# Joining layer 0's feed-forward and layer 1's attention rounds in one written program

## The chip, the core and the metric

The kernel runs on one core of one Trainium2 chip. The metric is the device time of one execution in microseconds (us). A core has five engines with a queue each: TensorE (PE in the profile; PEld is its loading of weights), VectorE (DVE), ScalarE (ACT), GpSimd (POOL) and SyncE (SP), which here mostly issues DMA transfers. Products land in PSUM, which has eight banks of 2 KB for each of the 128 partitions; everything else lies in SBUF. Shapes are written partitions x elements.

## The reference

A tensor x of 8 x 256 rows of 512 goes through two layers, each a normed attention on a context and a normed feed-forward, all added to x:

```python
x = x + _L0_xattn_ref(_layernorm(x), ctx, ctx, ...)     # retention, 4 heads
x = x + _L0_ffn_ref(_layernorm(x), w1, w2, w3)
x = x + _L1_xattn_ref(_layernorm(x), ctx, ctx, Wi, bi, Wf, bf, ln_scale)
x = x + _L1_ffn_ref(_layernorm(x), ...)                 # 32 experts, top 4, and a shared one
```

The change touches the second and the third line. The second, with hidden size 1408:

```python
def bitlinear(x, w):          # both sides rounded: x to 127 steps of its row's largest, w to -1, 0, 1
    return einsum('bsd,hd->bsh', act_quant(x), weight_quant(w))
h = silu(bitlinear(x, w1)) * bitlinear(x, w3)
return bitlinear(h, w2)
```

The third is an mLSTM of 16 heads of 32 (q is the normed x, k and v are the context):

```python
ig = (concat(q, k, v) @ Wi + bi);  fg = (concat(q, k, v) @ Wf + bf)     # one number per row and head
F = cumsum(log_sigmoid(fg))
log_D = F[s] - F[t] + ig[t]  for t <= s, else -inf;  M = max over t of log_D
C = (qh . kh / sqrt(32)) * exp(log_D - M)
h = (C / (max(|C.sum|, exp(-M)) + 1e-6)) @ vh
out = layernorm of each head of h, times ln_scale
```

## The kernel before

The 2048 rows are 16 tiles of 128 (two tiles are one of the 8 batches); x stays in SBUF as `g.X[0..15]`. `layers_kernel` (L1647) runs `layer0_attention`, then `layer1_constants` and `Gates` (weights and helpers of layer 1), `layer0_ffn`, `layer1_attention`, and `layer1_ffn` (routing and experts). The order of the work around the change is written out by hand: inside `tc.manual_schedule` the named engines get their instructions in the order of the program text (PE, ACT and DVE in the feed-forward; PE, ACT, DVE and POOL in layer 1's rounds), and other queues are ordered by a scheduler. Semaphores for data and for reused buffers are placed by the framework.

**`layer0_ffn` (L571)** loops over the 16 tiles t. Three chunks of hidden columns are 8 matmuls each (L590), into p1 and p3 (two PSUM buffers each); ACT makes silu (L598), DVE the gate (L603), its row's largest value (L607) and the rounding to bf16 (L626); a transposing DMA (L627) turns it; `output` (L632) is 11 matmuls for tile t-2; `added` (L637) puts it on x for tile t-3. For layer 1 each finished tile is then normed: `stats` (L109), an inverse root in about a dozen small DVE steps for a group of tiles (`rooted`, L89 to L102), `norm_next` on ACT (L696), four transposes on PE (`turn_next`, L704) into the bank `ft`, and a copy into `qT` (`copy_next`, L711). Groups of tiles for one root are 4, 2, 2, 4, 2, 1, 1. After the loop (L781 to L827) stands a tail: the last outputs and norms, and the gates of the later tiles.

**`Gates` (L449)** makes F, M and the rest for all rows at once, 128 pairs of batch and head on partitions. `context` (L491) multiplies the context's side in tiles 0 and 1, `queries` (L500) the side of q. `chain` (L509) is the sequence after that, for batches 0 to 3 (first) and 4 to 7 (second): products that pick the rows (L517), biases (L522, L525), log-sigmoid as Abs, Exp and Ln on ACT (L528 to L532), two scans (L537, L542), sums, then the split of two rows into three bf16 parts each (casts L552, subtractions L556), which go to DRAM (`parts_d`, L557; three `part` buffers), and a turned F (L563) whose Exp (L566) becomes `em`.

**`layer1_attention` (L861)** has 32 blocks (8 batches, 4 groups of 4 heads) and works on four at a time, one round per n (`round_`, L1102): `decays` of block n (products L909 and L910 of the operands `left` and `right` into one of two banks `dec`, then Exp L914 into `xe`, in three pieces), `back` of block n-3 (L965, copied by ACT into `hid`, L969), `weights` of n-1 (L929, L933, and DVE's product with the decays, `ct`, L937), `heads` of n-2 (L950; copy L958), and a `tail` that norms finished batches: absolute sums (L980, L981), squares on POOL (L987), variance (L993 to L995), the inverse root on DVE, scaling on POOL (L1000), `attended` on POOL (L1007, L1008: times ln_scale, added to x, one tile at a time), and later the norm for the next layer and its turned copy (`turned`, L1037, which also takes a `dec` bank). `hid` has three buffers, `xe` three. `values` (L882) loads the parts into `left` and `right` of one of two pairs, and the batch's context rows, at n % 4 == 2 for the next batch. The second chain of gates advances one step per round from round 0. Two lines that set the order of the tail of a batch (L1056 to L1060 and L1075):

```python
if r == 0: nm[b] = scales(..); sq[b] = squares(..); if b: attended(b - 1, hid.pop(b - 1), (1,))
if r == 3: ...; scaled(hid[b], rs); attended(b, hid[b], (0,) if b + 1 < B else (0, 1))
```

Block r of batch b here means round n = 4b + 6 + r.

Of the kernel before, what the change touches and what calls it, by code (L numbers as in the profile page):

```python
# [19 lines left out]
F32 = mybir.dt.float32  # L20
# [40 lines left out]
MAGIC = 12582912.0  # L61

# [386 lines left out]
class Gates:  # L449
# [4 lines left out]
    def __init__(self, g, wp):  # L454
        self.g = g
        nc = g.nc
        self.bif = wp.tile([P, 2], F32, tag="bif", name="bif")
# [8 lines left out]
        self.em = wp.tile([P, 2, P], F32, tag="em", name="em")  # L466
        self.parts = [wp.tile([P, S], BF16, tag=f"part{n}", name=f"part{n}") for n in range(3)]
# [4 lines left out]
        self.fg, self.af, self.ig, self.F, self.gg, self.M = (row() for _ in range(6))  # L472

# [10 lines left out]
    def open(self, ps):  # L484
        self.pg = ps.tile([P, CH], F32, tag="pg", name="pg", bufs=1)

    def context(self, of):

        for k in of:
            for c in range(NCH):  # L490
                self.g.nc.tensor.matmul(  # L491
                    self.pg[c * 2 * H1 : (c + 1) * 2 * H1, :], lhsT=self.Wkv[:, k, :], rhs=self.g.ctxT[c][:, k, :],
                    start=k == 0, stop=False,
                )

    def queries(self, of):

        for k in range(KD):
            for c, cols in of:
                self.g.nc.tensor.matmul(  # L500
                    self.pg[c * 2 * H1 : (c + 1) * 2 * H1, cols], lhsT=self.W[:, k, :], rhs=self.g.qT[c][:, k, cols],
                    start=False, stop=k == KD - 1 and cols.stop == CH,
                )

    def kept(self, h):
        rows = slice(h * 64, (h + 1) * 64)
        self.g.nc.vector.tensor_copy(self.gs[rows], self.pg[rows])

    def chain(self, h, two, turned, fine=False, each=False):  # L509
# [12 lines left out]
        nc.vector.tensor_scalar(fg, both[r, 1], self.bif[r, 1:2], None, ALU.add)  # L522
        if each:
            yield
        nc.vector.tensor_scalar(ig, both[r, 0], self.bif[r, 0:1], None, ALU.add)  # L525
        yield

        nc.scalar.activation(af, fg, AF.Abs)  # L528
        nc.scalar.activation(af, af, AF.Exp, scale=-1.0)
        if each:  # L530
            yield
        nc.scalar.activation(af, af, AF.Ln, bias=g.ones[r, 0:1])  # L532
        yield
        nc.vector.scalar_tensor_tensor(fg, fg, 0.0, af, ALU.min, ALU.subtract)
        if each:
            yield
# [3 lines left out]
        if each:  # L540
            yield
# [3 lines left out]
        if each:  # L545
            yield
        nc.vector.tensor_scalar(M, M, -1.0, None, ALU.mult)
        yield

        for n, rest in enumerate((gg, M)):  # L550
            for m, part in enumerate(self.parts):
                nc.vector.tensor_copy(part[r], rest)  # L552
                if each and m < 2:
                    yield
                if m < 2:
                    nc.vector.tensor_sub(rest, rest, part[r])  # L556
                (nc.sync if n or h else nc.scalar).dma_start(out=g.parts_d[n, m, r], in_=part[r])  # L557
                if (fine or each) and m < 2:
                    yield
            yield  # L560
# [6 lines left out]

# [3 lines left out]
def layer0_ffn(g, tc, gates):  # L571
# [5 lines left out]
    with tc.tile_pool(name="f0work", bufs=2, reuse_waits="tile") as work, tc.tile_pool(name="f0ps", bufs=2, space=PSUM, reuse_waits="tile") as ps:  # L577

        xq, h, p, am, inv, sc, hq, hqT, py, mv, var, roots, rs, nb, xn, ft = ({} for _ in range(16))

        def products(t, n):
            a, z = chunks[n]
            xqT = xq[t][0]
            if n == 0:
                h[t] = work.tile([P, FF], F32, tag="h", name="h")
            p1 = ps.tile([P, 512], F32, tag="p1", name="p1")
            p3 = ps.tile([P, 512], F32, tag="p3", name="p3")
            for pp, w in ((p1, w1), (p3, w3)):
                for k in range(KD):
                    nc.tensor.matmul(  # L590
                        pp[:, : z - a], lhsT=xqT[:, k, :], rhs=w[:, k, a:z], start=k == 0, stop=k == KD - 1
                    )
            sg = work.tile([P, 512], F32, tag="sg", name="sg")
            p[n] = p1[:, : z - a], p3[:, : z - a], sg[:, : z - a]
# [23 lines left out]
        def hidden_scale(t):  # L618
# [3 lines left out]
            hqT[t] = work.tile([P, NF, P], BF16, tag="hqT", name="hqT", bufs=3), s2  # L622

        def hidden_rounded(t):
            hq = work.tile([P, FF], BF16, tag="hq", name="hq")
            nc.vector.tensor_scalar(hq, h.pop(t), MAGIC, 127.0, ALU.subtract, ALU.min)  # L626
            nc.sync.dma_start_transpose(out=hqT[t][0], in_=hq)  # L627

        def output(t):
            py[t] = ps.tile([P, D], F32, tag="py", name="py")  # L630
# [8 lines left out]
        def input_normed(i):  # L639
            xn[i] = work.tile([P, D], F32, tag="y", name="xn")  # L640
# [8 lines left out]
        def input_rounded(i):  # L649
            q = work.tile([P, D], BF16, tag="xq", name="xq")  # L650
# [5 lines left out]
        groups = [range(4), range(4, 6), range(6, 8), range(8, 12), range(12, 14), range(14, 15), range(15, 16)]  # L656
# [3 lines left out]
        def stats(i):  # L660
            of = group[i]
            if i == of[0]:
                mv[of] = work.tile([P, 4, 2], F32, tag="mv4", name="mv4")
# [4 lines left out]
        def centers(of):  # L668
            m = len(of)
            v = work.tile([P, 4], F32, tag="var4", name="var4")[:, :m]  # L670
# [4 lines left out]
            nb[of] = work.tile([P, 4], F32, tag="nb4", name="nb4")[:, :m]  # L675
# [3 lines left out]
        def rooted(i, n):  # L679
            for _ in range(n):  # L680
                next(step.get(group[i], iter(())), None)

        def woven(i, others):
            for _ in others:
                rooted(i, 1)
            rooted(i, NT)
# [3 lines left out]
        def norm_next():  # L690
            if normed:
# [3 lines left out]
                y = work.tile([P, D], F32, tag="xn1", name="xn1")  # L695
# [3 lines left out]
        def turn_next(tag="ft", bufs=1):  # L699
            if turns:  # L700
                i, y = turns.pop(0)
                pt = ps.tile([P, KD, P], F32, tag=tag, name="ft", bufs=bufs)
# [4 lines left out]
        def copy_next():  # L707
            if copies:
                i, pt = copies.pop(0)
                c, o = divmod(i * P, CH)  # L710
                nc.scalar.copy(g.qT[c][:, :, o : o + P], pt)  # L711
                return i

        with tc.manual_schedule(engines={E_.PE, E_.Activation, E_.DVE}):
# [3 lines left out]
            gates.open(ps)  # L718
            at_py = lambda: ps.tile([P, 2, S], F32, tag="py", name="gates")
            first = gates.chain(0, at_py, at_py, each=True)  # L720

            for t in range(NT):
                front = t - 3
                if t:
# [6 lines left out]
                silu(t, 0)  # L731
                if t:
                    shifted(("h", t - 1), h[t - 1])
                gated(t, 0)
                if t + 2 < NT:
                    input_scale(t + 2)
                if front >= 0:
                    stats(front)
                    rooted(front, 2)
                products(t, 1)  # L740
                if t == NT - 1:
                    next(first)
# [3 lines left out]
                if front >= 0:  # L746
                    rooted(front, 3)
# [3 lines left out]
                if front >= 0:  # L751
                    rooted(front, 2)
                if t < 2:
                    gates.context(range(2 * t, 2 * t + 2))
                products(t, 2)
                silu(t, 2)
                if t == NT - 1:
                    for _ in range(4):
                        next(first)
                if t + 2 < NT:  # L760
                    input_rounded(t + 2)
                if front >= 0:
                    rooted(front, 2)
                turn_next()
                if t >= 2:
                    output(t - 2)
                gated(t, 2)
                if front >= 0:
                    rooted(front, NT)
                done = copy_next()  # L770
                if t + 3 < NT:
                    input_normed(t + 3)
                norm_next()
                largest(("h", t), h[t])
                if done == 7:
                    gates.queries([(0, slice(0, CH)), (1, slice(0, CH))])
                    gates.kept(0)

            last = NT - 1

            def steps(n):  # L781
                for _ in range(n):
                    yield next(first)

            hidden_scale(last)
            output(last - 1)
            turn_next()
            added(last - 2)
            shifted(("h", last), h[last])
            next(first)  # L790
            stats(last - 2)
            copy_next()
            norm_next()
            turn_next("p3", 2)
            hidden_rounded(last)
            rooted(last - 2, 2)
            added(last - 1)
            rooted(last - 2, 2)
            stats(last - 1)
            copy_next()  # L800
            norm_next()
            turn_next("p3", 2)
            copy_next()
            woven(last - 2, steps(6))
            output(last)
            norm_next()
            turn_next("p3", 2)
            norm_next()
            turn_next("ft")
            copy_next()  # L810
            copy_next()
            gates.queries([(2, slice(0, CH)), (3, slice(0, 2 * P))])
            woven(last - 1, steps(5))
            norm_next()
            turn_next("p3", 2)
            copy_next()
            gates.queries([(3, slice(2 * P, 3 * P))])
            added(last)
# [910 lines left out]
```

## Time and profile before

| what | us |
|---|---|
| median of 3 runs (1099.37 to 1104.2) | 1102.18 |
| the profiled execution | 1101.73 |
| its span | 1099.9 |
| feed-forward of layer 0, to its last products | 239.8 to 370.4 |
| from there to the first decay product | 370.4 to 403.0 |
| rounds 0 to 6 | 403.0 to 435.6 |
| rounds 7 to 13 | 435.6 to 465.8 |
| rounds 14 to 31 (the last Exp begins at 535.15) | 465.8 to 538 |

The mean granted clock of TensorE is 0.96. All times inside the program count from the span's start. One profiled execution has a page with busy time by engine and by slices; its trace answers questions by stretch of time, by wait and by instruction. In a row of the timeline the first number is the start, the second the busy time, then engine, line, operation, output and inputs, shapes, the count, and in brackets the idle time before it and what ended it. In a row of waits stand the engine and line that waited, what for, and the total, the number and the longest. In a row of stretches stand the stretch, its length, the busy time of PE, PEld, DVE, ACT and POOL with instruction counts, the granted clock, the DMA share and GB/s.

### The profile page before, as it was taken

The page shows a single profiled execution, that of the slowest core. Times are in us where ns is not written, and L with a number is a line of the kernel's source. Part 1 is how long each engine was busy: PE and PEld are TensorE (multiplying, and loading weights), DVE is VectorE, ACT ScalarE, POOL GpSimd, SP SyncE. Part 2 cuts the span into 40 slices and gives each one's busy share as a digit, 9 for nine tenths or more (in the row PEclk, how much of TensorE's full clock was granted, in tenths as well). Part 3 has the DMA queues.
Part 4 walks back from the last instruction along what each step waited for, and adds up shares of the span by engine and source line. Part 5 has one row for each costly group of instructions (what it writes and reads, how often), then busy time and mean ns, then how long its engine had stood idle before and what let it go on. Part 6 is the DMA issues. An engine that isn't in the chain of part 4 may idle for free.

```text
span 1099.9 us, 14847 instructions
## 1 busy us (share of the span) xinstructions
PE 1020.0 (93%) x5226; PEld 618.8 (56%) x5226; DVE 535.0 (49%) x1504; ACT 398.4 (36%) x680; POOL 395.5 (36%) x375
## 2 busy tenths in 40 slices
PE   7979799989999888999889899999999999999994
PEld 5746366634444345566534444555666666777782
DVE  6545555468999826888842992112221221121120
ACT  4455235136677536576631101221122222212211
POOL 0144522240000300376670223554455555545522
PEclk9989899999999868899989999999999999999997
DMA  9776321013234420212122325777777788889872
GB/s 342 275 274 216 131 93 48 1 30 59 55 70 56 117 68 27 77 61 71 39 88 81 128 84 162 177 200 189 174 199 203 203 207 235 228 226 252 239 198 35
DMA packets 101748, 154.42 MB, mean 140 GB/s; under 512 B 39812, under 2 KB 42500, under 8 KB 101640
## 3 DMA queue, kind: packets, MB, share of 16 engines
q1 hardware_dynamic: 81872, 106.68, 31.0%
q0 software_dynamic: 19552, 46.60, 19.0%
q8 instruction: 43, 0.70, 0.3%
q14 instruction: 41, 0.34, 0.1%
q10 hardware_dynamic: 240, 0.10, 0.0%
HBM read 110.42 MB, written 32.96 MB: 130 GB/s over the span
## 4 chain that ended last, share of the span: by engine, by line
PE 69%; DVE 13%; DMA 6%; POOL 4%; ACT 3%; issue 3%; SPq 0%; DVEq 0%; POOLq 0%; ACTq 0%
PE po L1478 13%; PE pg L1461 12%; PE pu L1461 12%; PE pz L380 3%; PE pw L325 3%; PE pt L1518 3%; PE p L590 3%; PE py L632 2%; DVE am L607 2%; PE pqk L929 2%; DMA vc_d<-raw 2%; PE pd L909 2%; PE num L950 2%; DMA raw<-in_ctx 1%; PE po L1168 1%
## 5 line engine op out<-in xcount | busy, mean ns | idle before, releaser
L1466 DVE TENSOR_TENSOR act<-pu,sg 128x264 f32<-128x264 f32 (+22 forms) x68 | 31.9, 469 | 314.7 <-PE pu L1461 308.5
L1503 POOL DMA_INDIRECT xg<-h_d,tok_of x85 | 83.3, 980 | 198.7 <-DVE of L1513 63.6
L1522 POOL DMA_INDIRECT out_x<-eo,to x85 | 133.0, 1564 | 54.9 <-ACT eo L1560 34.5
L1478 PE MATMUL po<-w,act 128*128 128x512 f32 (+10 forms) x456 | 143.1, 489 | 0.0
L1461 PE MATMUL pg<-xT,w 128*128 128x216 f32 (+21 forms) x512 | 136.5, 410 | 0.6 <-issue 0.6
L1461 PE MATMUL pu<-xT,w 128*128 128x216 f32 (+21 forms) x512 | 133.3, 403 | 0.0
L1560 ACT ACTIVATE eo<-po,slotw 128x512 f32<-128x512 f32 (+10 forms) x114 | 65.6, 576 | 176.9 <-PE po L1478 168.5
L1461 PEld LDWEIGHTS pg<-xT,w 128*128 128x128 f32 x512 | 93.9, 191 | 34.1 <-issue 18.7
L1461 PEld LDWEIGHTS pu<-xT,w 128*128 128x128 f32 x512 | 96.8, 190 | 26.2 <-issue 5.6
L1465 ACT ACTIVATE sg<-pg 128x264 f32<-128x264 f32 (+22 forms) x68 | 28.5, 419 | 204.5 <-PE pg L1461 192.3
L1478 PEld LDWEIGHTS po<-w,act 128*128 128x128 f32 (+10 forms) x456 | 54.1, 155 | 57.4 <-issue 47.9
L590 PE MATMUL p<-wq,xqT 128*128 128x512 bf16 (+1 forms) x384 | 80.3, 362 | 5.0 <-DVE qi L611 4.6
L937 DVE SCALAR_TENSOR_TENSOR ct<-pqk,xe 128x768 f32<-128x768 f32 x64 | 58.2, 951 | 21.7 <-PE pqk L933 16.7
L590 PEld LDWEIGHTS <-xqT 128*128 128x128 bf16 x384 | 37.2, 98 | 48.4 <-issue 10.1
L1519 DVE TENSOR_TENSOR xT<-pt,nw 128x512 f32<-128x512 f32 (+12 forms) x85 | 51.1, 601 | 21.0 <-PE pt L1518 20.8
L325 PE MATMUL pw<-wg,xnT 128*128 128x512 f32 x128 | 61.1, 622 | 0.0
L380 PE MATMUL pz<-wo,wyT 128*128 128x512 f32 x128 | 57.9, 595 | 2.1 <-ACT wyT L374 2.1
L914 ACT ACTIVATE xe<-pd 128x512 f32<-128x512 f32 x96 | 55.1, 596 | 11.0 <-PE pd L910 10.0
L1518 PEld LDWEIGHTS pt<-ident,xg 128*128 128x128 f32 (+15 forms) x340 | 39.2, 140 | 24.8 <-PE po L1478 10.5
L109 DVE BATCH_NORM_STATS2 st<-x 128x6 f32<-128x512 f32 x64 | 43.8, 685 | 15.8 <-POOL x L1008 10.2
L1518 PE MATMUL pt<-ident,xg 128*128 128x128 f32 (+15 forms) x340 | 47.2, 260 | 1.4 <-DMA xg<-h_d,tok_of 0.8
L363 POOL TENSOR_TENSOR y<-y,gam 128x512 f32<-128x512 f32 x16 | 20.9, 1304 | 76.0 <-DVE y L79 72.1
(295 smaller groups left out, 1671.1 us busy)
## 6 DMA issues: line engine op xcount, KB each, us to landing
w<-in_w SPq DMA_DIRECT2D x32, 1024.0 KB
w<-in_w SPq DMA_DIRECT2D x32, 512.0 KB
wst<-in_w1T SPq DMA_DIRECT2D x8, 704.0 KB
wst<-in_w3T SPq DMA_DIRECT2D x8, 704.0 KB
wst<-in_w2T SPq DMA_DIRECT2D x6, 768.0 KB
x<-in_x SPq DMA_DIRECT2D x16, 256.0 KB
ctxT<-in_ctxT_d SPq DMA_DIRECT2D x4, 1024.0 KB
raw<-in_ctx SPq DMA_DIRECT2D x16, 256.0 KB
```

The costliest lines, as they stand in the source:

```text
L325: nc.tensor.matmul(pw, lhsT=xnT[c][:, k, o : o + P], rhs=wg[:, k, :], start=k == 0, stop=k == KD - 1)
L380: nc.tensor.matmul(pz, lhsT=wyT[:, k, :], rhs=wo[:, k, :], start=k == 0, stop=k == KD - 1)
L590: nc.tensor.matmul(pp[:, : z - a], lhsT=xqT[:, k, :], rhs=w[:, k, a:z], start=k == 0, stop=k == KD - 1)
L914: nc.scalar.activation(out, pd, AF.Exp)
L937: nc.vector.scalar_tensor_tensor(ct[:, r : r + 2, :], pqk[:, :, : S + P], 1.0 / math.sqrt(HD1), xe[:, r : r + 2, :], ALU.mult, ALU.mult,)
L1461: nc.tensor.matmul(pp[:, :n], lhsT=w[:, k, cols], rhs=xT[:, k, :n], start=k == 0, stop=k == KD - 1)
L1478: nc.tensor.matmul(po[h * at : h * at + n, :cols], lhsT=act[:, m, j * P : j * P + n], rhs=w[:, m, h * cols : (h + 1) * cols], start=m == 0 ...
L1503: nc.gpsimd.indirect_dma_start(out=xg[:n], out_offset=None, in_=h_d, in_offset=bass.IndirectOffsetOnAxis(ap=g.tok_of[:n, r, j : j + 1], ax ...
L1518: nc.tensor.transpose(pt[:, k, :n], xg[:n, k * P : (k + 1) * P], g.ident[:n, :n])
L1519: nc.vector.tensor_mul(xT, pt[:, :, :n], g.nw.unsqueeze(2).to_broadcast([P, KD, n]))
L1522: return nc.gpsimd.indirect_dma_start(out=g.out, out_offset=bass.IndirectOffsetOnAxis(ap=rows, axis=0), in_=eo, in_offset=None, compute_op ...
L1560: nc.scalar.activation(eo[:n, at : at + cols], po, AF.Copy, scale=w[r][:n, j : j + 1])
```

## The change

`layer0_ffn` and `layer1_attention` become one function, `layers_joined`, with one SBUF pool and one PSUM pool for both; the round code moves to `layer1_rounds`. POOL and SP are now ordered by hand too. What was the feed-forward's tail stands in a table of places (round, place) inside rounds 0 to 6:

```diff
+            places = {
+                (0, 0): [partial(shifted, ("h", late), h[late]), partial(output, late - 1, "back", 1)],
+                (0, 1): [partial(hidden_rounded, late), partial(added, late - 1)],
+                (1, 0): [partial(rooted, 13, 6)],
+                (1, 3): [partial(rooted, 13), partial(stats, late - 1)],
+                (1, 4): [norms],
+                (2, 1): [turned],
+                (2, 3): [partial(output, late, "back", 1), rounds.second_right],
+                (2, 4): [partial(turned, nc.vector), partial(added, late), partial(times, 1, first), norms],
+                (3, 1): [partial(times, NT, first), turned],
+                (3, 3): [partial(stats, late)],
+                (3, 4): [partial(turned, nc.vector), norms],
+                (4, 1): [turned, partial(rooted, late, 6)],
+                (4, 3): [partial(rooted, late)],
+                (4, 4): [partial(turned, nc.vector)],
+                (5, 1): [norms],
+                (5, 4): [turned],
+                (6, 1): [turned],
+                (6, 4): [lambda: gates.late((2, 3), bank("dec", "pgl", 2))],
+            }
+            def between(n, place):
+                for work_of in places.get((n, place), ()):
+                    work_of()
+                if n >= 7 and place in (2, 4):
+                    times(3 if place == 2 else 2, second)
```

Places 0 to 4 of a round lie after the first two decay pieces, after `back`, after the third piece, after `weights`, and after `heads` with the tail. `turned` in this table is one tile's transposes into a `dec` bank and its copy, by ACT or DVE. `gates.late` is the query product of tiles 8 to 15 (8 matmuls of 512 columns).

The gates: the first chain's 15 steps to the last part stand in tiles 13 (3 steps), 14 (6) and 15 (6) of the feed-forward, the rest in rounds 2 and 3. Six part buffers take the place of three. The second chain waits until round 7 and then goes five steps a round. Log-sigmoid changes its form, and the second chain has a polynomial:

```diff
-        nc.scalar.activation(af, fg, AF.Abs)
-        nc.scalar.activation(af, af, AF.Exp, scale=-1.0)
-        nc.scalar.activation(af, af, AF.Ln, bias=g.ones[r, 0:1])
-        nc.vector.scalar_tensor_tensor(fg, fg, 0.0, af, ALU.min, ALU.subtract)
+        nc.scalar.activation(af, both[r, 1], AF.Tanh, bias=self.half[r, 0:1], scale=0.5)
+        nc.vector.tensor_scalar(fg, both[r, 1], self.bif[r, 1:2], 0.0, ALU.add, ALU.min)
+        nc.vector.tensor_scalar(ig, both[r, 0], self.bif[r, 0:1], None, ALU.add)
+        if h == 0:
+            nc.scalar.activation(af, af, AF.Abs)
+            nc.scalar.activation(af, af, AF.Ln, bias=self.half[r, 1:2], scale=0.5)
+            nc.vector.tensor_add(fg, fg, af)
+        else:
+            nc.scalar.activation(af, af, AF.Abs)
+            nc.vector.tensor_scalar(af, af, -0.5, None, ALU.add)
+            nc.vector.tensor_scalar(M, af, LOG[-1], None, ALU.mult)
+            for c in LOG[-2:0:-1]:
+                nc.vector.scalar_tensor_tensor(M, M, c, af, ALU.add, ALU.mult)
+            nc.vector.scalar_tensor_tensor(fg, M, LOG[0], fg, ALU.add, ALU.add)
...
-            layer1_constants(g, wp)
             gates = Gates(g, wp)
-            layer0_ffn(g, tc, gates)
-        layer1_attention(g, tc, gates)
+            layer1_constants(g, wp)
+            layers_joined(g, tc, qp, gates)
```

The buffers: p1 and p3 become one pair `p13` of two banks in the rounds' `pqk` (released together by the gate); `output` and the gates' products take the `dec` banks, `ft` takes `num` and `pg` takes `back`. In SBUF the hidden rows use the `xe` buffers, hq and its turned copy share the `ct` buffers. The first-layer weights wq0 and wq1 are reused after the feed-forward for two `hid` buffers (three before), `em`, the third `xe` and the squares; wq2, once output 15 is done, for the second right operand, which POOL clears and fills from the first, and for ln_scale:

```diff
-                        hid[b] = work.tile([P, 2, H1, HD1 + 1], F32, tag="hid", name="hid", bufs=3)
+            hid[b] = hid_of[b % 2]
...
+    def second_right():
+        more = qp.tile([P, NF * D // 2], F32, tag="wq2", name="held2")
+        half = KD * HG * S // 2
+        nc.gpsimd.memset(more[:, :half], 0.0)
+        right = more[:, :half].bitcast(BF16).rearrange("p (k r s) -> p k r s", k=KD, r=HG)
+        nc.gpsimd.dma_start(out=right[: 3 * HG], in_=g.right[0][: 3 * HG])
...
                     if r == 0:
                         nm[b] = scales(b, hid[b])
-                        sq[b] = squares(b, hid[b], nm[b])
                         if b:
                             attended(b - 1, hid.pop(b - 1), (1,))
+                        sq[b] = squares(b, hid[b], nm[b])
```

The first right operand is filled by four ACT copies in tiles 2 to 5 instead of eight POOL DMAs and a DVE cast; `values` loads the parts ahead of the context rows. The remaining moves in the feed-forward: context products in tiles 1 and 2, root groups 4, 4, 6, 2 with their steps spread over iterations, a tile's transposes split into two places of an iteration, hidden rows 13 and 14 rounded by ACT, `kept` on ACT, outputs 13, 14 and 15 in `num` and `back`.

## The prediction

> **What bounds the kernel now.** I read the page's slices first, then busy time by stage, then the waits of the joint, then two stretches in order of time. Three of the slices' rows (27.5 us a digit):
>
> ```profile
> PE   7979799989999888999889899999999999999994
> DVE  6545555468999826888842992112221221121120
> PEclk9989899999999868899989999999999999999997
> ```
>
> TensorE is nearly always busy; the one hole in its clock is slices 14 to 16, where the feed-forward ends and the rounds begin. By stage (sums of busy us, granted clock, DMA):
>
> ```profile
> core 0: us, PE busy (x) PEld busy (x) DVE busy (x) ACT busy (x) POOL busy (x), PEclk, DMA share, GB/s
> 239.80:370.40 130.60, 122.98 (x618) 58.59 (x617) 120.16 (x296) 84.32 (x111) 5.28 (x16) 0.99 0.34 59
> 370.40:403.00 32.60, 23.56 (x99) 12.35 (x98) 19.32 (x72) 16.41 (x23) 8.02 (x12) 0.72 0.39 120
> 403.00:435.60 32.60, 29.18 (x245) 15.63 (x245) 14.80 (x22) 19.02 (x36) 1.89 (x1) 0.75 0.12 30
> 435.60:465.80 30.20, 28.00 (x297) 17.43 (x296) 26.60 (x53) 16.74 (x39) 8.60 (x6) 0.89 0.24 69
> 465.80:538.00 72.20, 68.87 (x778) 44.81 (x780) 61.07 (x128) 52.03 (x115) 48.38 (x42) 1.00 0.19 62
> ```
>
> Row one, the feed-forward: PE and DVE both near full. Row two, the joint from the last products (370.4) to the first decay product (403.0): PE is busy 23.6 us but at clock 0.72. Row three, rounds 0 to 6: clock 0.75. Row four, rounds 7 to 13: DVE already holds 26.6 of 30.2 us. Row five, rounds 14 to 31: PE holds 68.9 of 72.2 us, so a PE wait there can hardly be made up. In the joint two engines wait for each other:
>
> ```profile
> ACT xn L696 <- DVE nb L676: 7.2, 3, 3.3
> PE ft L704 <- ACT xn L696: 5.9, 4, 2.0
> DVE part L552 <- DMA parts_d<-part: 5.8, 1, 5.8
> ```
>
> That is root, norm, transpose, copy, one tile after another, with 5.8 us in which DVE waits for a part buffer. This is what the change attacks.
>
> **The feed-forward: -2.5 us.** PE waits there 7.6 us: 2.6 (context products L491, whose weights come late), 4.6 for DVE in six pieces, 0.4 for ACT. Loading the gates' weights first and moving the context products a tile later takes the 2.6. Roots spread over iterations take perhaps 1.9 of the 4.6, and two fewer transposes of 0.44 take 0.9. Against that: the first chain now stands in tiles 13 to 15 on DVE, at 0.28 (cast, scalar), 0.42 (two operands), 0.66 (scan) about 6.8 us, while the rounding of hidden rows 13 and 14 leaves DVE (2 x 0.89) and input scaling has ended for the last two tiles (about 1.5 each): 2 us too much; pairing p1 with p3 costs one silu (0.65) at a refill. Sum -2.6 -1.9 -0.9 +2 +0.7, about -2.5; from -5 to +2. Last products end at 367.9.
>
> **The joint and rounds 0 to 6: 17.5 us gained, the FFN's 2.5 included.** Round 0 needs the first chain's parts in DRAM and back. DVE writes the last cast some 2.8 us after the last products (gate 0.6, parts 1.7, a root step): 370.7. Write to read took 1.9 us (cast end 395.74, load issued 397.60), a transfer 1.8 (388.94 to 390.76, the part's write); with the issue of 0.3 to 0.5, round 0 starts at 375 and not at 403. SP must not be blocked then: tile 14's transpose (2.1 us of issue) stands ahead of these loads and is over.
> From 375 to the start of round 7: seven rounds at the undisturbed pace of 3.38 (xe of rounds 4 to 11 start at 425.48, 428.86, 432.24 and so on) are 23.7. PE's moved work: outputs 14 and 15, 2 x 2.37; eight transposes of a tile, 8 x 0.5; eight query products of 512 columns, 2.4 (eight of 512 and eight of 256 took 3.62); F's transposes 0.5: 11.6. The clock: PE is idle from about 370.5 to 375, and comes back slow as at 403 (two stretches of 4 us at 0.50): 2. One root chain that ACT waits for, now in round 1: 2.7 to 3.3 in the joint's rows, take 3. Eight tiles pass through the two banks that the decays use; a turned tile there costs PE 0.35 today (idle ahead of 502.26 and of 506.57): 2.8. Sum 43.1, so round 7 starts at 418.1 instead of 435.6. Bounds: PE alone, 35.3, gives 25 gained; today's 32.6 for these rounds with 11.6 + 3 + 2.8 on top, 50, gives 10.5.
> What hides here costs nothing: four ACT copies for eight POOL DMAs and the heads' cast, the early memsets, POOL's 128x2048 clearing for the second right operand in round 2 (an estimate of 3.8 from 0.95 for a quarter of the bytes), since DVE holds 14.8 of 32.6 us there; without that cover it costs up to 3.8. The Ln and Exp loads of round 2 (413.09 and 414.91, 1.28 each, with PE waiting 3.3) go; their place is in the 3.38.
> The Trainium skill, "ScalarE: Activation LUTs", "What ACT_TABLE_LOAD costs", gives about 2.66 us a switch, a drain included; here the next activation starts 0.02 us after a load of 1.28 and I see no drain. By the page the two loads would be worth 5.3 us, by the row 2.6.
>
> **Rounds 7 to 13: 6.4 us lost.** The second chain is no longer spread from round 0: all of it stands in rounds 7 to 11, with a polynomial in place of Exp and Ln. On DVE: five scalar steps 1.4, eight polynomial steps 3.4, one sum 0.4, scans 1.3, two more 0.8, parts 3.4: 10.8, of which the parts (3.4) stand in this window today. So 26.6 + 7.4 = 34.0 us of DVE; with 2.6 us of gaps (3.6 today) 36.6 against 30.2. Lower bound 3.8 (no gaps). Upper bound 9: DVE's steps also stretch beside POOL, which this window shows:
>
> ```profile
> 448.22 1.96 POOL L1000 TENSOR_TENSOR hid<-hid,rsq 128x1024 f32<-128x1024 f32 x1 [12.65 <-DVE rsq L102]
> 448.44 2.02 DVE L556 TENSOR_TENSOR sw<-sw,part 64x256 f32<-64x256 f32 x1
> ```
>
> The subtraction that takes 0.42 elsewhere took 2.02 beside POOL's product. That now can strike any of 28 steps.
>
> **Rounds 14 to 31: 17 us lost.** Three hid buffers become two. The copy into batch b+2's first block (round 4b+11) must then wait until POOL has added batch b's second tile. Batch 3 today:
>
> ```profile
> 500.94 1.91 POOL L1000 TENSOR_TENSOR hid<-hid,rsq 128x1024 f32<-128x1024 f32 x1
> 502.94 1.18 POOL L1007 TENSOR_TENSOR hid<-hid,lns 128x512 f32<-128x512 f32 x1
> 503.29 0.38 ACT L969 COPY hid<-back 128x264 f32<-128x264 f32 x1
> 504.19 1.19 POOL L1008 TENSOR_TENSOR x<-x,hid 128x512 f32<-128x512 f32 x1
> 505.33 1.90 POOL L987 TENSOR_TENSOR sq<-hid 128x1024 f32<-128x1024 f32 x1
> 507.19 1.18 POOL L1007 TENSOR_TENSOR hid<-hid,lns 128x512 f32<-128x512 f32 x1
> 508.44 1.19 POOL L1008 TENSOR_TENSOR x<-x,hid 128x512 f32<-128x512 f32 x1
> ```
>
> Today the copy of 503.29 is batch 5's and goes to a third buffer. With two it waits for batch 3's last add. The change puts that tile ahead of the squares, so the add ends at 505.4 + 2.4 = 507.85 and not 509.6: ACT stands 4.55 us. Behind the copy on ACT: the third Exp, the head's copy, the turned tile's copy, the next round's Exps. PE goes on with weights, heads and the turned tile (to 505.9); then both decay banks are held, and the next decay product waits for the third Exp to end, 507.95 + 0.4 + 0.6 = 508.95: 3.05 us. Some comes back (DVE's 1.65 us idle at 502.9 and a slow round 24 leave about 1.2; take 0.6). The clock: after PE's pause at 453 to 456, beside POOL, it was granted 0.50 in 455 to 458 and 0.66 in 458 to 461, some 1.9 us of work lost; taken by half, 1.0. So 3.45 a batch, in rounds 15, 19, 23, 27 and 31: 17.3 (round 11's falls where DVE bounds). Bounds: 0 if POOL is done in time, 25 at 5 each.
> "TensorE: Matmul & The Clock Gate", "HAM oscillation", says in the Trainium skill that idle gaps past about 3.4 us put the clock at half. A pause of 3.05 lies just under it: by the rule 0 for the clock, or about 1.7 if the pause is a bit longer; the row's pause was near 3 and did cost clock.
>
> **After round 31** the routing and experts have the same instructions; the chain of waits there hangs on nothing that changed: 0.
>
> **Sum.** -17.5 + 6.4 + 17.3 = +6.2. The profiled execution took 1101.73 us (span 1099.9 and 1.8 around it; the median of the runs shown, 1102.18, lies 0.45 above): 1107.9, **1108**.
>
> **Rivals.**
> (A) *The third buffer isn't missed* (chance 0.25): faster. If the third Exp's bank isn't what PE needs next, or POOL's batch work starts a round earlier against PE, the wait stays on ACT and costs 1 us a batch. For: ACT holds only 52 of 72 us there. Against: PE's next instruction in order is that decay product, with two banks only. Then -17.5 + 6.4 + 5 = -6, 1096; with the full 25 of the first term 1088. It decides where a batch loses under 2.3 us.
> (B) *The joint doesn't close* (0.2): the decays' two banks, through which outputs, tiles and gates go too, make ACT and PE alternate, or the parts come late because SP or DVE is behind in tile 15. For: DVE is 95% full in the feed-forward; ACT's work in rounds 0 to 6 rises from 19 to about 28 us. Then 10 or less is gained: 1115, and with rounds 7 to 13 at 9, 1118 to 1124.
> (C) *Forecast* (0.55): all three terms near their size, 1099 to 1115, its own range.
>
> **How the numbers follow.** Half a per cent, 5.5 us, is about what a measurement of this kernel can tell from no change. Faster by more: A, 0.25. Slower: B and the upper part of C, 0.2 + 0.35 = 0.55. Within: 0.2. The range reaches from A with some of its larger gain to B: 1089 to 1124.
>
> **What would show it.** Right: the first xe near 375; round 7 at 415 to 422; DVE full in rounds 7 to 12; in rounds 15, 19, 23, 27 and 31 a wait of 4 to 5 us of ACT's hid copy for POOL, with a PE wait of some 3 us for xe after it. Wrong: no such PE wait (A); a first xe after 380, or PE waiting over 10 us in rounds 0 to 6 (B); a round of 3.4 us in 7 to 11 (the polynomial hidden).

## The result, and the profile after

The changed kernel takes 1119.12 us (median of 4 runs, 1117.76 to 1120.59), the kernel before 1103.19 (4 runs): ratio 1.0149, 95% interval 1.0115 to 1.0182. The forecast was 1108, in a range of 1089 to 1124, with 0.55 on slower: the side and the range held, and the time lies 11 us above the forecast, in the range of rival B.

The profiled execution has a span of 1118.5 us, against 1099.9. The same three rows of the page's slices (28 us a digit now):

```profile
PE   7979899989999589778798898999999999999994
DVE  6545645469997546966752794121211212111220
PEclk9989899999999789888999899999999999999997
```

The hole of slices 14 to 16 (counted from 0) has become a dent in slice 13 and a long stretch of 7 and 8, with some 9, behind it, to slice 24. By stage (stretch, length, busy PE, PEld, DVE, ACT, POOL with counts, clock, DMA, GB/s):

```profile
239.80:368.00 128.20, 120.39 (x603) 57.28 (x613) 116.12 (x271) 91.35 (x119) 5.58 (x17) 1.00 0.33 56
368.00:379.80 11.80, 3.39 (x13) 1.40 (x12) 6.41 (x14) 3.81 (x5) 0.00 (x0) 0.71 0.39 93
379.80:428.00 48.20, 37.83 (x302) 20.80 (x302) 21.31 (x51) 24.74 (x46) 4.91 (x4) 0.86 0.17 40
428.00:469.10 41.10, 33.99 (x304) 21.46 (x305) 35.00 (x71) 18.35 (x41) 9.38 (x6) 0.83 0.08 21
469.10:552.90 83.80, 70.32 (x742) 43.60 (x741) 56.87 (x127) 49.39 (x110) 45.67 (x40) 0.88 0.22 72
```

The joint (row two) is 11.8 us and no longer 32.6. But rounds 0 to 6 (row three) take 48.2 us for 37.8 of PE work, rounds 7 to 13 (row four) 41.1 for 34.0, and the rounds after that (row five), full before, leave PE idle for 13 us and its clock at 0.88. In the waits of the joint and rounds 0 to 6 the part buffers' wait is gone, and three others stand there:

```profile
PE pd L680 <- DMA right<-parts_d: 8.4, 1, 8.4
PE ft L1150 <- ACT held L685: 4.5, 1, 4.5
ACT xn L1142 <- DVE nb L1127: 3.5, 1, 3.5
```

PE waits 8.4 us until the parts are back from DRAM; in round 2 its transposes wait 4.5 us for Exps, which on ACT stand behind norms that wait 3.5 us for a root.

To compare kernels I cut every profiled execution at the same five events. The start differs by up to 6 us among kernels whose instructions are the same up to there, so a stage says more than the total (us; t0 is the feed-forward's first product, r0, r7 and r14 the first Exp of a round, "routing" POOL's first instruction of the routing; differences of times rounded to 0.1, so a last digit can be off by one):

| kernel | t0 | t0 to r0 | r0 to r7 | r7 to r14 | r14 to routing | routing to end | span | ratio to before (95%) |
|---|---|---|---|---|---|---|---|---|
| before | 239.8 | 164.1 | 31.8 | 30.2 | 107.4 | 526.7 | 1099.9 | |
| changed | 238.1 | 141.7 | 48.2 | 41.1 | 124.4 | 525.0 | 1118.5 | 1.0149 (1.0115 to 1.0182) |
| e1 scaling apart | 243.3 | 143.9 | 47.4 | 41.5 | 123.0 | 524.9 | 1124.0 | 1.0190 (1.0170 to 1.0210) |
| e2 no second chain | 241.9 | 141.9 | 48.4 | 28.8 | 121.7 | 522.5 | 1105.1 | 1.0068 (1.0042 to 1.0094) |
| e3 chain 7 a round | 243.5 | 142.1 | 47.6 | 45.8 | 125.0 | 522.1 | 1126.0 | 1.0249 (1.0227 to 1.0272) |
| e4 before, two hid | 240.2 | 163.8 | 31.7 | 29.6 | 122.4 | 523.3 | 1110.9 | 1.0120 (1.0095 to 1.0145) |
| e5 e1, variance later | 243.3 | 142.0 | 48.1 | 41.7 | 117.2 | 524.8 | 1117.1 | 1.0151 (1.0115 to 1.0188) |
| e6 chain around POOL | 240.3 | 141.9 | 47.7 | 38.2 | 126.4 | 522.5 | 1116.9 | 1.0197 (1.0159 to 1.0235) |
| e7 root in one piece | 244.0 | 143.3 | 41.0 | 41.1 | 123.3 | 522.0 | 1114.7 | 1.0131 (1.0087 to 1.0175) |
| e8 parts by SP, early Exp | 240.4 | 140.0 | 47.4 | 41.0 | 123.2 | 522.1 | 1114.1 | 1.0146 (1.0104 to 1.0187) |
| e9 three hid, two xe | 239.0 | 143.4 | 47.1 | 43.3 | 110.0 | 525.6 | 1108.4 | 1.0083 (1.0050 to 1.0115) |
| e10 e5 to e8 together | 240.7 | 140.1 | 41.4 | 40.0 | 120.9 | 523.5 | 1106.5 | 1.0050 (1.0031 to 1.0070) |
| e11 e6 to e9 together | 239.0 | 140.0 | 42.1 | 41.6 | 110.5 | 525.4 | 1098.7 | 1.0026 (1.0008 to 1.0044) |
| e12 e11 with Ln | 239.7 | 138.6 | 45.5 | 39.3 | 109.9 | 526.0 | 1098.9 | 0.9999 (0.9977 to 1.0021) |

Changed less before, stage by stage: -1.7 - 22.4 + 16.4 + 10.9 + 17.0 - 1.7 = 18.5 us.

### The profile page after: what moved, and what is told of

Read it like the earlier page. It is cut to its first block, busy times and chain, and to the rows that moved or that the text cites. A ratio compares the mean times of both kernels' runs of the same rounds, so it can differ in the third digit from the quotient of the medians.

```text
span 1118.5 us, 14696 instructions
## 1 busy us (share of the span) xinstructions
PE 1017.1 (91%) x5196; PEld 617.7 (55%) x5210; DVE 531.9 (48%) x1474; ACT 399.6 (36%) x682; POOL 393.1 (35%) x371
## 4 chain that ended last, share of the span: by engine, by line
PE 65%; DVE 17%; POOL 7%; DMA 4%; issue 3%; ACT 3%; SPq 0%; POOLq 0%; DVEq 0%; ACTq 0%
PE po L1536 13%; PE pg L1519 12%; PE pu L1519 12%; PE pz L384 3%; PE pw L329 3%; PE pt L1576 3%; DVE ct L708 3%; PE p L1036 2%; DVE am L1053 2%; DVE h L1049 2%; DMA raw<-in_ctx 2%; PE py L1083 1%; POOL x L779 1%; POOL held L778 1%; PE po L935 1%
## 5 line engine op out<-in xcount | busy, mean ns | idle before, releaser
L1536 PEld LDWEIGHTS po<-w,act 128*128 128x128 f32 (+10 forms) x456 | 54.1, 154 | 57.5 <-issue 47.6
L1576 PEld LDWEIGHTS pt<-ident,xg 128*128 128x128 f32 (+15 forms) x340 | 39.1, 140 | 24.8 <-PE po L1536 10.5
L708 DVE SCALAR_TENSOR_TENSOR ct<-pqk,xe 128x768 f32<-128x768 f32 x44 | 40.2, 952 | 24.3 <-PE pqk L704 16.1
```

The costliest lines, as they stand in the source:

```text
L708: nc.vector.scalar_tensor_tensor(ct[:, r : r + 2, :], pqk[:, :, : S + P], 1.0 / math.sqrt(HD1), xe[:, r : r + 2, :], ALU.mult, ALU.mult,)
L1536: nc.tensor.matmul(po[h * at : h * at + n, :cols], lhsT=act[:, m, j * P : j * P + n], rhs=w[:, m, h * cols : (h + 1) * cols], start=m == 0 ...
L1576: nc.tensor.transpose(pt[:, k, :n], xg[:n, k * P : (k + 1) * P], g.ident[:n, :n])
```

## The experiments

Two theories were to be told apart for the late rounds: the two hid buffers, or only the new order of POOL's work. For rounds 7 to 13: DVE's load, its stretching beside POOL, or the hid wait of round 11. For the joint: the two decay banks, or the order in which parts and roots arrive.

**e4, the kernel before with two hid buffers and the new order of POOL's work.**

```diff
-                        hid[b] = work.tile([P, 2, H1, HD1 + 1], F32, tag="hid", name="hid", bufs=3)
+                        hid[b] = work.tile([P, 2, H1, HD1 + 1], F32, tag="hid", name="hid", bufs=2)
...
-                        sq[b] = squares(b, hid[b], nm[b])
                         if b:
                             attended(b - 1, hid.pop(b - 1), (1,))
+                        sq[b] = squares(b, hid[b], nm[b])
```

> The kernel before with two hid buffers instead of three and the second tile's addition ahead of the squares, nothing else of the change. Theory: the wait is a matter of the two buffers alone and costs 3 to 4 us in each of rounds 15 to 31 and some in round 11: 1117 to 1122. Rival, it needs the joined program around it: under 5 us, 1103 to 1108.

r14 to routing grows from 107.4 to 122.4, nearly as in the changed kernel (124.4), and no other stage moves by more than 3.4. Waits of e4 from round 14 on:

```profile
ACT hid L969 <- POOL x L1008: 22.2, 5, 5.0
PE pd L909 <- ACT xe L914: 11.7, 4, 3.7
```

Five waits of ACT's copy for POOL, and PE waits for decay banks behind it: the loss needs nothing of the change but these two edits. (The total, 1114.53, is below the 1117 to 1122 expected; the last stage was 3.4 shorter.) No run has the new order with three buffers, so what the order costs by itself stays open. That it isn't free shows in another wait: DVE's variance waits 12.5 us in five times for POOL's squares here, 0.6 us in the kernel before. In the changed kernel one of the five waits of the copy, in round 23, in order of time:

```profile
517.28 0.66 PE L808 MATMUL hT<-ident,yn 128*128 128x128 f32 x4
518.52 1.17 POOL L779 TENSOR_TENSOR x<-x,held 128x512 f32<-128x512 f32 x1
519.73 0.38 ACT L740 COPY held<-back 128x264 f32<-128x264 f32 x1 [4.30 <-POOL x L779]
520.66 0.58 PE L680 MATMUL pd<-right,left 128*128 128x512 bf16 x1 [2.72 <-ACT held L685]
```

The copy starts as POOL's last add of batch 3 ends, the third Exp follows, and PE goes on after 2.7 us. It is the copy of the same batch that the prediction read in the kernel before.

**e1, POOL's scaling apart.** It writes into the squares' tile, so hid is free once it is read.

```diff
-        nc.gpsimd.tensor_mul(flat(hid), flat(hid), rs.unsqueeze(2).to_broadcast(shape))
+        y = squared.rearrange("p (n d) -> p n d", d=HD1)
+        nc.gpsimd.tensor_mul(y, flat(hid), rs.unsqueeze(2).to_broadcast(shape))
+        return y
...
-                scaled(hid[b], rs[:, :NV])
+                hid[b] = scaled(hid[b], rs[:, :NV])
```

> Theory, the two hid buffers: POOL's scaling writes into the squares' tile and no longer in place, so hid is free about 5 us earlier in each batch; same instructions, same order. ACT's hid copies wait for POOL no more (22.0 us in five waits before), four rounds take 16.5 us again and not 20.4, from round 15 on: 17 to 20 us less than the changed kernel, 1099 to 1102. Rival, the order: the squares now come after the second tile's addition, DVE's variance comes 3 us later, and that is what slows a batch: at most 5 us less, 1114 or more.

A miss: 123.0 from r14 to routing, 1.4 saved. The copies' waits for POOL's adds are gone from the list, the rounds between stalls are back to 16 or 17 us for four, but a new wait stands in rounds 17 and 25, and the end after the last Exp grew. Round 17:

```profile
488.81 1.22 DVE L765 TENSOR_REDUCE var<-held 128x32 f32<-128x1024 f32 x1 [3.64 <-POOL held L758]
491.25 0.71 PE L700 MATMUL pqk<-qT,ctxT 32*128 32x256 f32 x4 [3.19 <-DVE ct L708]
```

DVE's reduction waits 3.64 us for POOL's squares (L758), which now come after two operations on the other tile; the product with the decays is queued behind it on DVE, and PE stands 3.19 us. The rival was right about this half: the buffer and the order are two waits on the same 9 us of POOL work, and taking away one uncovers the other.

**e5, the variance a round later as well.**

```diff
-            if r == 1:
-                v[b] = g.small.tile([P, NV + 4], F32, tag="var", name="var")
-                variance(v[b][:, :NV], sq.pop(b), nm.pop(b))
...
             if r == 2:
+                variance(v[b][:, :NV], sq.pop(b), nm.pop(b))
                 roots[b] = rsqrt(g, v[b], NV + 4)
```

> The scaling written apart, as in the first run, and DVE's variance a round later, so that no product with the decays is queued behind the wait for POOL's squares. Theory, both waits come from POOL's work on one batch (the copy's for the buffer, and in its place DVE's reduction for the squares): round 14 to the last Exp takes 70 to 73 us (89.8 in the changed kernel, 81 with the scaling apart alone). Rival, the stalls of rounds 17 and 25 of that run had another cause (loads of weights and context rows): 78 to 82 us.

77.8 to the last Exp, just under the rival's range and above the theory's; 117.2 to routing, 7.2 better than the changed kernel. Both waits for POOL are gone from the list, and what remains is a round of 5.8 us in most batches (once 8.3) in which variance and root together stand on DVE before the product. Moving the work inside two buffers gives back less than half.

**e9, a third hid buffer in the place of the third xe buffer, POOL's order as before.**

```diff
-        if (b * KD + k) % 3 < 2:
-            xe = work.tile([P, HG, S + P], F32, tag="xe", name="xe")
-        else:
-            xe = third
+        xe = work.tile([P, HG, S + P], F32, tag="xe", name="xe")
...
-            hid[b] = hid_of[b % 2]
+            hid[b] = hid_of[b % 3]
```

> The changed kernel with a third hid buffer in the place of the third xe buffer, and the order of POOL's work as before the change (squares, then the second tile). Theory, the third hid buffer is what rounds 14 to 31 lack: round 14 to the last Exp takes 70 to 74 us (89.8 in the changed kernel, 70.9 before); the stretch behind it, which the waits had shortened, comes back to 563, so the kernel gains 10 to 14, not 18. Rival, the third xe buffer was as needed (an Exp must wait until DVE has used the block before last): 78 us or more.

110.0 to routing: 14.4 of the 17.0 us are back, and the clock of the late rounds is 1.00 again. Round 14 to the last Exp takes 74.4, just above the theory's range and far from the rival's. The price of having two xe buffers is 3.5 us there against the kernel before (rounds of 4.1 to 4.5, once 5.6, where that has 3.4 to 5.0), and 2.2 us in rounds 7 to 13, where the Exps now wait for DVE:

```profile
ACT xe L682 <- DVE ct L705: 8.3, 2, 7.3
```

So the third buffer, with the order that goes with it, is what the late rounds lacked.

**e2, no second chain.** Its steps are left out, and batches 4 to 7 take the first chain's parts.

```diff
-                if n >= 7 and place in (2, 4):
-                    times(3 if place == 2 else 2, second)
```

> Leaves out the second chain of gates (batches 4 to 7 take the first chain's parts and maxima). Theory, DVE's load and its stretching beside POOL: rounds 7 to 13 fall from 41 us to 28 to 31, the kernel to 1106 to 1109. Rival, the hid wait of round 11 makes rounds 7 to 13 long: they fall by 5 us or less, 1114 or more.

Rounds 7 to 13 fall from 41.1 to 28.8, below the 30.2 of before, though round 11 still has its hid wait. The chain costs 12.3 us there. Round by round, changed against e2, 4.0 of it stand in round 7 (7.8 against 3.8) and 4.9 in round 11 (11.7 against 6.8), the rest in small pieces. In round 7 of the changed kernel:

```profile
429.65 1.94 PE L535 MATMUL gates<-sw 64*64 64x256 f32 x8
431.63 0.47 ACT L541 ACTIVATE sw<-gates,bif 64x256 f32<-64x256 f32 x1 [1.27 <-PE gates L535]
432.13 0.49 DVE L542 TENSOR_SCALAR sw<-gates,bif 64x256 f32<-64x256 f32 x1 [3.83 <-ACT sw L541]
433.08 0.71 PE L700 MATMUL pqk<-qT,ctxT 32*128 32x256 f32 x4 [0.63 <-DVE sw L544]
```

The chain begins with eight products on PE, in one of the two `pqk` banks that the round's own products use; ACT and DVE stand idle until they are there, and the clock falls to half from 434.4 to 437.8. At the end of round 9:

```profile
447.31 2.09 POOL L771 TENSOR_TENSOR held<-held,rsq 128x1024 f32<-128x1024 f32 x1 [23.26 <-DVE rsq L106]
447.65 2.29 DVE L562 TENSOR_TENSOR_SCAN sw<-ones,sw 64x256 f32<-64x256 f32 x1
449.98 1.22 DVE L564 TENSOR_TENSOR sw<-sw 64x256 f32<-64x256 f32 x1
451.23 1.55 DVE L566 TENSOR_TENSOR_SCAN sw<-sw 64x256 f32<-64x256 f32 x1
452.81 1.22 DVE L568 TENSOR_TENSOR sw<-sw 64x256 f32<-64x256 f32 x1
455.08 1.67 PE L700 MATMUL pqk<-qT,ctxT 32*128 32x256 f32 x6 [5.68 <-DVE ct L708]
```

Two scans and two sums that take 0.69 and 0.42 alone (e3's, before POOL starts) take 6.3 us in all, and PE waits 5.7.

**e3 and e6, where the chain stands against POOL.** e3 takes seven steps a round; e6 puts 19 steps into rounds 7 to 9, none into 10 and 11, and the rest into 12 and 13.

```diff
-                    times(3 if place == 2 else 2, second)
+                    times(4 if place == 2 else 3, second)
```

> The second chain goes seven steps a round in place of five, so its two scans and two sums stand ahead of POOL's work on batch 0. Theory, stretching beside POOL: these four fall from 6.3 us to 2.2 and the kernel gains 3 to 5, 1114 to 1116. Rival, DVE's load alone: the same work in the same rounds, 1118 to 1121.

```diff
+            steps = {(7, 2): 3, (7, 4): 2, (8, 2): 4, (8, 4): 4, (9, 2): 6, (12, 2): 3, (12, 4): 3, (13, 2): 3}
...
-                if n >= 7 and place in (2, 4):
-                    times(3 if place == 2 else 2, second)
+                times(steps.get((n, place), 0), second)
```

> The changed kernel with the second chain's steps kept out of rounds 10 and 11: 19 steps in rounds 7 to 9, ahead of POOL's work on batch 0, the parts in rounds 12 and 13 behind it. Theory, DVE's operations on SBUF last as long as POOL's beside them: rounds 7 to 13 take 33 to 36 us (41.1). Rival, the load of DVE alone: 39 to 42 us.

Neither reading of e3 held: its rounds 7 to 13 are 4.7 us longer than the changed kernel's (its span 7.5, of which 5.4 are the start). The four steps did fall to 2.2 us, but the parts moved into POOL's 9 us, and with them the transposes that PE has in order; these take a `pqk` bank, which the product with the decays (`ct`), queued on DVE behind the parts, must first leave:

```profile
454.71 1.95 POOL L771 TENSOR_TENSOR held<-held,rsq 128x1024 f32<-128x1024 f32 x1 [25.52 <-DVE rsq L106]
454.81 2.00 DVE L577 CAST sw<-sw 64x256 bf16<-64x256 f32 x1
456.85 1.35 DVE L579 TENSOR_TENSOR sw<-sw 64x256 f32<-64x256 f32 x1
466.38 0.47 PE L584 MATMUL pmT<-ident,sw 64*128 64x64 f32 x2 [9.91 <-DVE ct L708]
```

A cast of 0.29 takes 2.00, one step per POOL operation, and PE waits 9.9 us. In e6 no step is stretched, and the stage still takes 38.2, between the two readings: 2.9 saved of 12.3. DVE's busy time in rounds 7 to 13, without the chain (e2) and with it unstretched (e6; its last four steps fall just behind the window):

```profile
432.10:460.90 28.80, 25.31 (x295) 15.68 (x295) 19.30 (x42) 16.44 (x38) 8.44 (x6) 0.94 0.08 24
429.90:468.10 38.20, 32.38 (x304) 19.71 (x305) 28.60 (x65) 18.05 (x42) 8.43 (x6) 0.87 0.07 19
```

DVE is idle 9.6 us of e6's 38.2, so its load as a sum doesn't set the stage. What is left stands in round 7 (8.1) and in round 10 (8.9): ten chain steps, 4.9 us, stand on DVE ahead of round 9's product, PE waits 2.96 for it, and has half clock from 449.7 to 456.5. And the next stage loses 2.0, which I put down to the parts that leave late. SP's queue in e6:

```profile
462.43 7.95 SPq L580 DMA_DIRECT2D parts_d<-sw  x6
470.48 1.12 SPq L652 DMA_DIRECT2D left<-parts_d  x3
```

Batch 4's operands are only asked for at 470.5, two us into round 14.

**e7, the root in one piece; e8, parts by SP and an early Exp.**

```diff
-                (1, 0): [partial(rooted, 13, 6)],
-                (1, 3): [partial(rooted, 13), partial(stats, late - 1)],
+                (1, 0): [partial(rooted, 13)],
+                (1, 3): [partial(stats, late - 1)],
```

> The root of tiles 8 to 13 stands whole at the start of round 1, ahead of the first product with the decays, not half of it behind. Theory, ACT's norms held back the Exps of round 2 until the root was done, and PE waited 4.5 us and came back at half clock: first Exp to round 7 takes 43 to 45 us (48.2). Rival, the two decay banks are the limit and the wait comes back elsewhere: 47 to 49 us.

```diff
-                (nc.sync if n or h else nc.scalar).dma_start(out=g.parts_d[n, m, r], in_=part)
+                nc.sync.dma_start(out=g.parts_d[n, m, r], in_=part)
...
+            early = g.small.tile([P, 1], F32, tag="early", name="early", bufs=1)
+            nc.scalar.activation(early, g.ones[:, 0:1], AF.Exp)
             hidden_scale(late)
```

> The first three parts go out by SP in place of ACT, and one Exp of a single column ahead of the loop loads ACT's table while it waits. Theory: silu of the last tile no longer stands 2.9 us behind ACT's issuing, and 1.28 us of table load goes off the path: last products to first Exp falls by 2 to 4 us from 13.0 (366.8 to 379.8). Rival, the read of the parts sets it anyway: within 1 us.

e7 moves a few DVE steps of 0.17 us ahead of one product, and rounds 0 to 6 fall from 48.2 to 41.0, more than expected (the eight kernels with the root as changed take 47.1 to 48.4 there, the four with it in one piece 41.0 to 45.5). e8: from the start of the last product to the first Exp 9.9 us, against 13.2 to 13.6 in all kernels with the joint as changed. In the changed kernel ACT's queue had shown it:

```profile
366.34 2.00 ACTq L580 DMA_DIRECT2D parts_d<-sw  x3
368.44 0.69 ACT L1044 ACTIVATE sg<-p,s 128x512 f32<-128x512 f32 x1 [2.90 <-DMA parts_d<-sw]
```

e8 has two edits, and no run tells what each is worth. The totals don't show either gain: against the kernel before, run beside them, the ratios are 1.0131 and 1.0146, and the changed kernel's 1.0149 lies within both intervals. In e7's profiled execution the start took 5.9 us more (244.0 and not 238.1).

**e10, e11, e12, together.** e10 joins e5 to e8, e11 joins e6 to e9, and e12 is e11 with `if h in (0, 1):` ahead of the Ln branch and the steps {(7, 2): 3, (8, 2): 3, (8, 4): 3, (9, 2): 6, (12, 2): 3}.

> The scaling apart and the variance later, the chain around POOL, the root in one piece, the parts by SP and the early Exp together. If the stages add up: 140 to the first Exp, 41 to round 7, 37 to 39 to round 14, 78 to the last Exp: 18 to 22 us less than the changed kernel, 1097 to 1102. If they eat each other's gain: over 1105.

> The third hid buffer in the place of the third xe, the chain around POOL, the root in one piece, the parts by SP and the early Exp together. If the stages add up: 140, 41, 36 to 38, 71 to 74, and 563 behind: 1088 to 1096, ahead of the kernel before by 3 to 12. If DVE is late for the second xe buffer in rounds 7 to 13: 1100 or more.

> The last combination with the second chain's log-sigmoid by ACT's Ln, as in the first chain, in place of DVE's polynomial, and its steps in rounds 7 to 9 and 12. Theory, the load of DVE in rounds 7 to 9: 4.2 us of polynomial less, round 7 to 14 takes 36 to 38 us (41.6 with the polynomial), the kernel 1098 to 1100. Rival, two table loads of 1.28 us among the Exps cost as much as the polynomial: 41 us or more, 1102 to 1105.

e10, at 1107.4, falls short of its sum by some 5 us, in rounds 7 on. e11, at 1103.3, has nearly the expected stages but for rounds 7 to 13: 41.6, no better than the changed kernel, as foreseen for a DVE that is late for the second xe buffer; ACT's Exps wait 9.3 us for DVE there. With Ln (e12, 1101.6, between its two readings) that stage is 39.3, 2.3 better and not 4. Rounds 0 to 6 were 3.4 longer in e12's execution than in e11's. The program is the same there, and so are the busy times of all engines but TensorE; the clock isn't (e11, then e12; it is third from the end):

```profile
379.00:421.20 42.20, 34.40 (x305) 19.09 (x305) 21.44 (x51) 24.79 (x47) 4.90 (x4) 0.97 0.18 46
378.30:423.70 45.40, 38.03 (x306) 21.09 (x305) 21.39 (x51) 25.00 (x46) 4.90 (x4) 0.89 0.17 42
```

Why it was granted less in that execution isn't shown. By the runs e11 is 0.3% slower than the kernel before and e12 equal to it. In e11's profile, against before, the joint wins 24.1 us, rounds 0 to 6 pay back 10.3, rounds 7 to 13 11.4 and the rounds to the routing 3.1; no version here beats the kernel before.

## Why the prediction was right, and where it was not

The side and the range held, but not in the way of the forecast. C, with 1099 to 1115 as its own range, asked for all three terms near their size, and one was. The 1119 measured is the time of rival B (1118 to 1124, with 10 or less gained in the joint and 9 lost in rounds 7 to 13), to which I had given 0.2. Its signs nearly came as well: the first Exp at 379.8 (B: after 380), PE idle 10.4 us in rounds 0 to 6 (B: waits over 10), round 7 at 428.0 and not by 422.

**Right: rounds 14 to 31, 17 us lost.** Measured 17.0 to the routing, by the mechanism foreseen: ACT waits 4.3 us for batch 3's add in round 23 (foreseen 4.55), PE 2.7 (3.05), and e4 and e9 pin it to the buffer and its order together. The clock, taken by half, did fall. Stretches around the pause of round 23 (the granted clock is third from the end):

```profile
514.00:518.00 4.00, 3.63 (x44) 2.40 (x44) 2.23 (x4) 1.36 (x3) 3.84 (x4) 1.00 0.04 16
518.00:522.00 4.00, 1.18 (x4) 0.36 (x4) 1.62 (x4) 2.27 (x6) 3.47 (x3) 0.71 0.00 0
522.00:526.00 4.00, 4.00 (x28) 2.66 (x30) 1.20 (x3) 2.36 (x5) 0.41 (x1) 0.50 0.01 4
```

Rival A is refuted: the wait did reach PE. That the sum fits so well is in part luck. Four rounds from 14, 18, 22 and 26 on take 5.4, 4.3, 4.1 and 1.6 us more than before, not 3.45 each: three of these PE pauses (3.95, 2.36 and 2.72 us) went with half clock, the fourth (2.48, in round 27) didn't. And the pause near 3 from which I took the clock's price isn't in the row: in the kernel before PE's pauses there are 1.13 us (to 451.51) and 1.07 us (to 455.81).

**Mis-sized: the joint and rounds 0 to 6, 17.5 foreseen, 6.0 measured** (-22.4 + 16.4), outside my bounds of 10.5 to 25. Two terms failed. The first Exp came 6.5 us later after t0 than foreseen (141.7 against 375 - 239.8 = 135.2). The last cast ended 4.8 us after the last products and not 2.8, with the last tile's silu 2.9 behind ACT's issuing of parts. I priced write to read at 1.9 and the transfer at 1.8 from rows where SP had two stores and two loads ahead of the load. Measured were 3.7 from the end of the last cast (371.65) to the issue of the last load (375.36), since SP issues three parts, three left loads and the right one in turn, and 2.2 for the load. I also left out a table load of 1.28 (378.50). e8, which takes ACT's issuing and this load off the path, gains 3.4. The second term, 3 us for a root that ACT waits for, left out who stands behind ACT: the Exps of round 2, hence PE, hence its clock (0.72 in 388 to 400). e7 puts that at 7.2. Of rival B's two causes the two banks aren't it: with the root moved, rounds 0 to 6 take 41.0, under my 43.1 with the same banks. The other, parts that come late, is: SP's and ACT's issuing holds them.

**Mis-sized: rounds 7 to 13, 6.4 foreseen, 10.9 measured**, above my upper bound of 9. DVE was busy 35.0 us, near the 34.0 of the sum, but by luck: without the chain it is busy 19.3 (e2), not the 23.2 that I had left of today's 26.6, and the chain's steps, 10.8 in the sum, take 15.4 with their stretching beside POOL, which I had kept for the upper bound. It was idle for 6.1 and not 2.6. The failed step is that I summed DVE's load and left out what waits in order: the chain's products on PE in round 7 (4.0 us in that round), and four steps ahead of a round's product that fall together with POOL's burst and with round 11's hid wait (4.9), which I had put down as hidden by DVE. That e6 comes to 38.2, near my 36.6, is no support for the sum, since DVE is idle 9.6 us in it.

**The feed-forward** gained 0 to 2 us (128.4 to 130.3 from t0 to the last product's start, 130.3 before), with 2.5 foreseen.

## What to carry to other kernels

When memory forces one buffer fewer, replay one period on the waiting engine and on the two behind it: that sum came out right here, though the single batches did not, and a cure that frees the buffer but keeps the order only moved the wait to the next consumer of the same engine. When a chain of small steps is moved, price not its load but its place: which larger operation of another engine each step would run beside, and which in-order queue stands behind each step that waits. And a serial joint that is folded into a loop brings its own latencies along (a store, a load, a table, a root); count each of them again behind the queue that it will have there.

## What the runs showed of the hardware

In these stretches DVE's small operations between two places in SBUF last about as long as the POOL operation beside them: a cast of 0.29 took 2.00, a scan of 0.69 took 2.29, a subtraction of 0.42 took 1.35, while the product with a PSUM input (`ct`, 1.82 for two) stayed at 1.82 in the same stretch. The Trainium skill names this: "GPSIMD Engine Reference", "1. Specifications", says that POOL shares its SBUF interfaces with VectorE and contends with DVE's instructions that have two SBUF inputs or run in a 2-port mode. The runs agree for the scans, sums and subtractions, which have two such inputs (in which mode the cast ran isn't shown), and add that the DVE step ends shortly after POOL's operation does, 0.1 to 0.6 us in the rows of e3 and the changed kernel.

A PE pause of 2.7 us, shorter than the limit of the page that the prediction named, was enough for half clock over the next 4 us and more; so was one of 2.36 in round 19. One of 2.48 in round 27 was not: the clock stayed at 1.00 in 540 to 544 and 542 to 546.
